# Layer 1 of a four-layer graph network: seven node tiles instead of six from neighbour lists for the last two batches, and their projections between quarters of the scored sums

## The chip, the cores and the metric

The kernel runs on one core of a Trainium2 chip. The core has five engines that work side by side, each with its own queue in which it goes in order: TensorE (PE, matrix products; its weight loads are shown apart as PEld), VectorE (DVE), ScalarE (ACT), GpSimd (POOL) and SyncE (SP, which here issues DMAs). They wait for each other by semaphores. The metric is the device time of one execution, in microseconds, as a median over several executions.

## What is computed

16 batches of N = 1024 nodes with D = 256 features pass four graph layers, all float32. The adjacency `adj` (1024 x 1024) is symmetric in its pattern and sparse: a node has a link to itself and to each other node with a chance of about 1.6%.

```python
# layer 0, per batch; U = h @ W1[:d], V = h @ W1[d:]
S = sigmoid(relu(U[u] + V[v] + b1) @ W2 + b2)            # one score per pair of nodes
a = (S * adj).T @ h ;  m = (adj.T @ h) * h
h = beta1*h + beta2*(a @ Wa + ba) + beta3*(m @ Wm + bm)
# layer 1
h = h + relu((adj @ h) @ W.T + b)
# layers 2 and 3, attention
feats = h @ W1.T ;  f = feats @ W2 + b2
h = softmax(leaky_relu(f[:, None] + f[None, :]) + adj) @ feats + bias2 + h
```

## The kernel before: how the work is tiled and ordered

**State and tiles.** The node state `z` of a batch lies feature-major in SBUF: 128 partitions x 2 feature halves x 1024 nodes. A node tile is P = 128 nodes, so there are NT = 8. Batches go in groups of GB = 4; there are NGR = 4 groups, `g` = 0 to 3. `product` (L131) is the one place that issues matrix products; one float32 product shows as two PE records, each with a weight load. A transpose by PE is one record.

**Layer 0** needs scores for linked pairs only. Neighbour lists name up to FIRST = 16 neighbours per node in a first table, and NG = 4 references to extra rows for nodes with more; the extra rows stand in XT = 6 tiles of 128 rows of QUAD = 4 neighbours each. Scores are worked out from gathered rows on POOL, DVE and ACT, in the background of PE's work on earlier groups (`side`), and put into a dense array in DRAM.

**The scored sums** of a group are in `with_edges` (L1118). They go over four quarters of the columns (QN = 256 nodes). A quarter takes eight PSUM banks `acc` (4 batches x 2 feature halves), loads a block `gd` of scores for each of eight node tiles, turns it into batch-major form `gc` (ACT L1133 for even tiles, DVE L1131 for odd), and issues eight products for each. At the quarter's end eight DVE additions (L1156) put the sums onto `z`. PSUM has eight banks in all, handed out in turn.

**Layer 1** for two batches at a time (`layer_one`, L1205): `projected` (L1161) makes `y` = `z` @ W.T node-major, in four steps of two node tiles (a step is two batches x two tiles x two feature halves = 8 products, 16 PE records), each bank copied out by ACT (L1174). `neighbours` (L1189) then sums `adj` @ `y` over a range of columns: for each of eight node tiles it loads a strip `adjT_in` by SP (L1195, three buffers) and issues four products. `onto` (L1181) applies relu on ACT (`r`, L1186) and adds to `z` on DVE (L1187).

**Layers 2 and 3** for two batches at a time (`pair_layers`): `front` makes `feats` and the two factors of the exponentials; `sums` builds for each node tile a weight matrix `m` by one DVE instruction (L1099), and issues four products with it; `second` and `third` scale by the row sums (reciprocal `share` on DVE, L1276 and L1330), turn back by transposes (L1289, L1316) and add.

**The last group's last two batches.** After `with_edges` of group 3, `far_ahead` (L1405) runs. It first projects batches 14 and 15 (`z[2:]`), and as each bank is copied out, SP stores it to `y_d` in DRAM (L1408; eight stores). From then on two things go side by side:
- the main line: `rest`, which is `neighbours` for batches 14 and 15 over the node columns from FAR x 128 on, then all layers of batches 12 and 13 (`pair_layers` with `layer_one`);
- `by_lists` (L1210), which makes the layer 1 sums of batches 14 and 15 for the first FAR node tiles from the neighbour lists: no PE, but for each list position a gather of 128 rows of 512 values from `y_d` by POOL (in `gather`, L708) and a DVE step that adds the scaled row to `msg` (L1246 for the first position, L1248 for the others). First come the 6 x 4 = 24 extra-row steps (`x_node`), whose sums `part` are stored by SP to `part_d` (L1252). Then come 16 steps for each of the FAR tiles, and last four steps for each tile that gather from `part_d` and add with an L1244 instruction.

Gathers run LEAD = 4 steps ahead of the DVE step that uses them, into slot buffers of which there are six. `slots` sets the pace: the generators of the main line yield their nominal PE time, and for each us of it 0.68 steps of `by_lists` are issued up to 82 us, and 0.61 after that. A DVE step made by `paced` also waits for the sixth-last PE product before it. Afterwards `from_lists` (L1255) turns `msg` back by transposes (L1265, four for each tile), `onto` adds it, and batches 14 and 15 go through layers 2 and 3, up to the kernel's end.

So the order on each engine is that of the program text after this interleaving; each engine goes through its own queue in order.

Of the kernel before, what the change touches and what calls it, by code (L numbers as in the profile page):

```python
# [29 lines left out]
NG = EXTRA // QUAD  # L30
XT = 6
HOLD = 40
FAR = 6
AHEAD = 3
LEAD = 4
TOP = 16.0
# [34 lines left out]
def gnn_stack_kernel(  # L71
# [616 lines left out]
    with tc.If(listed > 0) as arm:  # L688
        with ExitStack() as stack:
# [427 lines left out]
            def exponential(jt):  # L1117
                paced(nc.scalar.activation(ea[:, jt, :], ea[:, jt, :], AF.Exp), 16)  # L1118

            def with_edges(g, hw, z):  # L1120

                doing[0] = "edges"
                for v in range(N // QN):
                    cols = slice(v * QN, (v + 1) * QN)
                    acc = [[bank() for _ in range(DH)] for _ in range(GB)]
                    for ut in range(NT):
                        gd = first_gd.pop(0) if first_gd else load_gd(g, v, ut, back=BACK)
                        gc = gc_pool.tile([P, GB, QN], F32, tag="gc", name="gc")
                        by_batch = gd.rearrange("p n i -> p i n")
                        if ut % 2:  # L1130
                            paced(nc.vector.tensor_copy(gc, by_batch), 16)  # L1131
                        else:
                            paced(nc.scalar.activation(gc, by_batch, AF.Copy), 16)  # L1133
                        for i in range(GB):
                            for eh in range(DH):
                                product(
                                    acc[i][eh][:, :QN], hw[i][:, ut, eh * P : (eh + 1) * P], gc[:, i, :],
                                    start=ut == 0, stop=ut == NT - 1,
                                )
                        if z_loads and ut % 2 == 0:  # L1140
                            load, i = z_loads.pop(0)
                            paced(load(i), 12)
                        if (to_load or to_exp) and ut % 2 and v:
                            if v > 1 and to_exp:
                                exponential(to_exp.pop(0))
                            if to_load:
                                jt = to_load.pop(0)
                                paced(nc.sync.dma_start(ea[:, jt, :], adjT_d[jt]), 16)
                                to_exp.append(jt)
                        yield 3.4 if g or v else 1  # L1150
                    if v == N // QN - 1:
                        while to_exp:
# [8 lines left out]
            def projected(z, keep=None):  # L1161

                doing[0] = "one"
                y = [node_major("y") for _ in range(2)]
                for jt in range(0, NT, 2):
                    for i in range(2):
                        ps = bank()
                        for k in range(2):
                            for dh in range(DH):
                                product(  # L1170
                                    ps[:, k * D : (k + 1) * D], z[i][:, dh, (jt + k) * P : (jt + k + 1) * P],
                                    l1wT[:, dh, :], start=dh == 0, stop=dh == DH - 1,
                                )
                        nc.scalar.activation(  # L1174
                            y[i][:, jt : jt + 2, :], ps.rearrange("p (t d) -> p t d", t=2), AF.Copy
                        )
                        if keep:
                            keep(i, slice(jt, jt + 2), y[i][:, jt : jt + 2, :])
                        yield 1.7
                return y  # L1180

            def onto(z, cols, sums):
# [6 lines left out]
            def neighbours(y, z, cols):  # L1189
                doing[0] = "one"  # L1190
                n = cols.stop - cols.start
                acc = [[bank() for _ in range(DH)] for _ in range(2)]
                for jt in range(NT):
                    a = three.tile([P, HN], F32, tag="a", name="adjT_in")[:, :n]
                    nc.sync.dma_start(a, adjT_d[jt][:, cols])  # L1195
                    for i in range(2):
                        for eh in range(DH):
                            product(
                                acc[i][eh][:, :n], y[i][:, jt, eh * P : (eh + 1) * P], a,
                                start=jt == 0, stop=jt == NT - 1,  # L1200
                            )
# [9 lines left out]
            def by_lists(msg):  # L1211

                spares = [gd_pool.tile([P, QN, GB], F32, tag="gd", name="msg") for _ in range(4)]
                halves = [
                    t.rearrange("p n i -> p (n i)")[:, k * 2 * D : (k + 1) * 2 * D] for t in spares for k in range(2)
                ]
                msg.extend(halves[:FAR])
                part = halves[FAR:]
                nc.gpsimd.memset(part[0], 0.0)
                nc.sync.dma_start(part_d[XT * P :, :], part[0])  # L1220

                nc.vector.tensor_scalar(to_u, to_u, float(XT * P), None, ALU.min)
# [12 lines left out]

                for step in todo[:LEAD]:
                    fetch_row(*step)
                for n, (t, k) in enumerate(todo):
                    if n + LEAD < len(todo):
                        fetch_row(*todo[n + LEAD])  # L1240
                    z = got.pop((t, k))
                    to = msg[t] if t < NT else part[t % len(part)]
                    if t < NT and k >= FIRST:
                        paced(nc.vector.tensor_tensor(to, to, z, ALU.add))  # L1244
                    elif k == 0:
                        paced(nc.vector.tensor_scalar(to, z, lists(t)[3][:, k : k + 1], None, ALU.mult))  # L1246
                    else:
                        paced(nc.vector.scalar_tensor_tensor(  # L1248
                            to, z, lists(t)[3][:, k : k + 1], to, ALU.mult, ALU.add
                        ))  # L1250
# [173 lines left out]
            for g in range(NGR):  # L1424
                hw, z = loaded.pop(0)
                while g not in finished:
                    next(side.steps)
                side.along(with_edges(g, hw, z))
                if g < NGR - 1:
                    side.along(group_layers(g, z))  # L1430
                else:
                    for _ in far_ahead(z[2:], pair_layers(g * GB, z[:2], layer_one(z[:2]))):
# [134 lines left out]
```

## Time and profile before

| what | value |
|---|---|
| median of 6 executions | 3139.49 us (3132.43 to 3148.79) |
| the profiled execution: its time | 3140.89 us |
| the profiled execution: its span | 3139.1 us |
| mean granted TensorE clock in it | 0.996 |
| PE `gc,hw` products of group 3 end | 2724 us after the span's start |
| projections of batches 14 and 15 on PE | 2723.95 to 2737.8 us |
| `rest` (256 columns) on PE | 2737.8 to 2752.3 us |
| layer 1 of batches 12 and 13 on PE | 2752.3 to 2828.8 us |
| layers 2 and 3 of batches 12 and 13 on PE | 2828.8 to 2979.9 us |
| turning `msg` back on PE (24 transposes) | 2979.9 to 2982.5 us |
| first gather from `y_d`, last gather from `part_d` (POOL) | 2741.5 and 2970.6 us |

The profile is of one execution. Times are in microseconds from the start of its span; a line names engine, line of the kernel, operation, the buffers that it writes and reads, and how often. "Idle before" is the time in which the engine did nothing just ahead of the instruction, and the name behind the arrow is what released it ("issue" is no wait that the profile shows). In rows of groups the columns are: count, busy time, mean duration in ns, idle time before with its releasers.

### The profile page before, as it was taken

The numbers are of one execution on the slowest core, as the hardware profiler recorded it, in microseconds if no ns is written. First come the engines' busy times: TensorE is split into PE (matmuls) and PEld (weight loads), VectorE is DVE, ScalarE is ACT, GpSimd is POOL, SyncE is SP. The second block draws the span as 40 slices with busy tenths as digits, with TensorE's granted clock in tenths as the row PEclk, the third lists the DMA queues.
The fourth block names the chain that finished last, engine by engine and source line by source line (L and its number), as shares of the span: only waits on it lengthen the run. The fifth ranks groups of instructions, "written<-read, shape, count | busy, mean of one in ns | idle before, by whom it ended". The sixth has DMA issues, their size and how long they took to land. (4 is left out here: it accounts for less than half of the span.)

```text
span 3139.1 us, 39040 instructions
## 1 busy us (share of the span) xinstructions
PE 3080.7 (98%) x11954; PEld 2185.0 (70%) x11954; DVE 2423.3 (77%) x3247; ACT 1822.7 (58%) x6456; POOL 1886.3 (60%) x1483
## 2 busy tenths in 40 slices
PE   9999999999999999999999999999999999999999
PEld 5544544545547756888885688888568888858888
DVE  7887768678776779989887899988789982257844
ACT  3345555566665776767666677776667762214242
POOL 1156777676665677657667766667777651066600
PEclk9999999999999999999999999999999999999999
DMA  9998898888889777558877755797775564485500
GB/s 319 331 332 303 274 294 273 262 248 256 253 285 337 229 222 209 152 147 270 290 227 222 225 150 158 264 300 241 223 205 150 164 210 153 132 253 161 161 4 28
DMA packets 288420, 699.96 MB, mean 223 GB/s; under 512 B 46141, under 2 KB 141178, under 8 KB 281034
## 3 DMA queue, kind: packets, MB, share of 16 engines
q0 software_dynamic: 128224, 387.80, 42.3%
q1 hardware_dynamic: 132538, 258.46, 23.6%
q10 hardware_dynamic: 27440, 51.13, 4.3%
q8 instruction: 96, 1.57, 0.2%
q14 instruction: 122, 1.00, 0.1%
HBM read 565.83 MB, written 131.41 MB: 222 GB/s over the span
## 5 line engine op out<-in xcount | busy, mean ns | idle before, releaser
L831 ACT ACTIVATE z<-z 128x256 f32<-128x256 f32 x2432 | 979.3, 406 | 587.1 <-DVE z L827 507.8
L825 DVE TENSOR_TENSOR z<-z,u 128x1024 f32<-128x1024 f32 x608 | 737.5, 1219 | 301.4 <-PE bank L131 178.5
L131 PE MATMUL bank<-feats,m 128*128 128x257 f32 x4096 | 910.3, 380 | 5.5 <-ACT st L1329 4.6
L708 POOL DMA_INDIRECT z<-v_d,slot_v x512 | 662.5, 1294 | 385.0 <-ACT z L831 198.2
L131 PEld LDWEIGHTS bank<-feats,m 128*128 128x128 f32 x4096 | 770.6, 190 | 116.2 <-ACT st L1329 5.4
L713 POOL DMA_INDIRECT dense_d<-gt,slot_at x512 | 677.1, 1322 | 199.0 <-issue 140.9
L827 DVE SCALAR_TENSOR_TENSOR z<-z,w2r 128x1024 f32<-128x1024 f32 x608 | 737.1, 1219 | 9.3
L131 PE MATMUL bank<-gc,hw 128*128 128x256 f32 x2048 | 454.8, 383 | 19.4 <-ACT gc L1133 12.1
L831 ACT ACTIVATION_READ_ACCUMULATOR z<-z 128x1 f32 x2432 | 460.5, 189 | 0.6 <-issue 0.6
L131 PEld LDWEIGHTS bank<-gc,hw 128*128 128x128 f32 x2048 | 389.6, 192 | 84.1 <-ACT gc L1133 15.6
L131 PE MATMUL bank<-adj_sb,h 128*128 128x512 f32 x1024 | 442.4, 592 | 3.8 <-ACT st L333 1.9
L1099 DVE SCALAR_TENSOR_TENSOR m<-rho,tau,adj_sb 128x512 f32<-128x512 f32 x512 | 375.5, 742 | 69.7 <-PE bank L131 65.2
L131 PE MATMUL bank<-adjT_in,y 128*128 128x512 f32 (+1 forms) x960 | 401.4, 578 | 2.7 <-DMA adjT_in<-adjT_d 2.3
L131 PEld LDWEIGHTS bank<-adj_sb,h 128*128 128x128 f32 x1024 | 194.2, 190 | 243.5 <-issue 238.2
L131 PE MATMUL bank<-w,hT 128*128 128x512 f32 (+1 forms) x1024 | 335.0, 487 | 0.0
L131 PEld LDWEIGHTS bank<-adjT_in,y 128*128 128x128 f32 x960 | 181.6, 190 | 216.0 <-issue 204.0
L131 PEld LDWEIGHTS bank<-w,hT 128*128 128x128 f32 x1024 | 194.8, 191 | 141.5 <-issue 122.3
L1133 ACT ACTIVATE gc<-gd 128x1024 f32<-128x1024 f32 x64 | 132.9, 2077 | 178.9 <-PE bank L131 117.9
L131 PE MATMUL bank<-g_wT,z 128*128 128x257 f32 x1024 | 230.1, 380 | 0.0
L131 PEld LDWEIGHTS bank<-g_wT,z 128*128 128x128 f32 x1024 | 192.2, 190 | 30.0 <-issue 2.9
L708 POOL DMA_INDIRECT z<-v_d,x_node x96 | 126.3, 1316 | 121.6 <-ACT z L831 64.3
L1131 DVE COPY gc<-gd 128x1024 f32<-128x1024 f32 x64 | 71.4, 1116 | 109.4 <-PE bank L131 76.3
(169 smaller groups left out, 2442.9 us busy)
## 6 DMA issues: line engine op xcount, KB each, us to landing
gd<-dense_d SPq DMA_DIRECT2D x128, 512.0 KB
dense_d<-zero ACTq DMA_DIRECT2D x64, 512.0 KB
adjT_in<-adjT_d SPq DMA_DIRECT2D x112, 256.0 KB
h<-in_x_dram SPq DMA_DIRECT2D x19, 1024.0 KB
u_d<-st SPq DMA_DIRECT2D x64, 256.0 KB
v_d<-st SPq DMA_DIRECT2D x64, 256.0 KB
hw_d<-st SPq DMA_DIRECT2D x64, 256.0 KB
u<-u_d POOLq DMA_DIRECT2D x32, 512.0 KB
```

Source lines behind the costliest of these rows:

```text
L131: recent.append(nc.tensor.matmul(*args, **kw))
L708: return nc.gpsimd.indirect_dma_start(out=dst, out_offset=None, in_=src[:], in_offset=bass.IndirectOffsetOnAxis(ap=at, axis=0), **how,)
L713: return nc.gpsimd.indirect_dma_start(out=dst[:], out_offset=bass.IndirectOffsetOnAxis(ap=at, axis=0), in_=src, in_offset=None,)
L825: paced(nc.vector.tensor_tensor(z, z, u, ALU.add))
L827: nc.vector.scalar_tensor_tensor(zk, zk, 0.0, w2r[:, None, :].to_broadcast([P, GB, D]), ALU.max, ALU.mult)
L831: nc.scalar.activation(zk[:, c, :], zk[:, c, :], AF.Copy, accum_out=s[:, k, c : c + 1])
L1099: nc.vector.scalar_tensor_tensor(m, r[:, cols], ta[:, kt : kt + 1], ea[:, kt, cols], ALU.max, ALU.mult)
L1131: paced(nc.vector.tensor_copy(gc, by_batch), 16)
L1133: paced(nc.scalar.activation(gc, by_batch, AF.Copy), 16)
```

## The change

1. FAR goes from 6 to 7: seven node tiles of batches 14 and 15 come from lists, and `rest` has 128 columns instead of 256. That is 20 more gathers and DVE steps (16 from `y_d`, 4 from `part_d`), and 28 transposes in `from_lists`, whose second group has 384 columns instead of 256.
2. The two `part` tiles, which were spare halves of the four `msg` buffers, lie in a buffer of the `gc` pool.
3. The order of steps: for each tile its 16 rows from `y_d` and then its four from `part_d`, instead of all tiles' rows first and all parts last.
4. The stores of `part` to `part_d` are issued three steps later than the step that completes them.
5. The pace is 0.75 steps for each nominal us throughout.
6. The projection becomes a class whose `y` lies in two halves of node tiles (each for both batches) instead of one buffer for each batch. In group 3, `with_edges` gets it as `between`: projection step 0 runs after the second quarter, step 1 after the third, each with its two `y_d` stores. Steps 2 and 3 run at the start of `far_ahead`, after the fourth quarter.

```diff
-FAR = 6
+FAR = 7
...
-            def with_edges(g, hw, z):
+            def with_edges(g, hw, z, between=None):
...
+                    if between and 0 < v < N // QN - 1:
+                        yield from between(v - 1)
+
+            class Projection:
+                def __init__(self, z, keep=None):
+                    self.z, self.keep, self.halves = z, keep, []
+
+                def __call__(self, i, jt):
+                    return self.halves[jt // HT][:, i, jt % HT, :]
+
+                def pair(self, q):
+                    if q % 2 == 0:
+                        t = ttile("y")[:, : 2 * HT * D]
+                        self.halves.append(t.rearrange("p (i t d) -> p i t d", i=2, t=HT))
                     for i in range(2):
                         ps = bank()
                         for k in range(2):
+                            jt = 2 * q + k
                             for dh in range(DH):
                                 product(
...
+                        at = 2 * q % HT
+                        y = self.halves[-1][:, i, at : at + 2, :]
+                        nc.scalar.activation(y, ps.rearrange("p (t d) -> p t d", t=2), AF.Copy)
+                        if self.keep:
+                            self.keep(i, slice(2 * q, 2 * q + 2), y)
                         yield 1.7
...
-                part = halves[FAR:]
+                free = gc_pool.tile([P, GB, QN], F32, tag="gc", name="part").rearrange("p i n -> p (i n)")
+                part = [free[:, : 2 * D], free[:, 2 * D :]]
...
-                todo += [(t, k) for t in range(FAR) for k in range(FIRST)]
-                todo += [(t, FIRST + q) for t in range(FAR) for q in range(NG)]
-                got = {}
+                todo += [(t, k) for t in range(FAR) for k in range(FIRST + NG)]
+                got, done = {}, []
...
                     if t >= NT and k == QUAD - 1:
-                        nc.sync.dma_start(part_d[(t - NT) * P : (t - NT + 1) * P, :], to)
+                        done.append((n + 3, t - NT, to))
+                    if done and n == done[0][0]:
+                        _, at, of = done.pop(0)
+                        nc.sync.dma_start(part_d[at * P : (at + 1) * P, :], of)
...
-            def far_ahead(z, main):
-                both = y_d.rearrange("(t p) (i d) -> p t i d", p=P, i=2)
-                y = yield from projected(z, lambda i, ts, y: nc.sync.dma_start(both[:, ts, i, :], y))
+            def far_ahead(z, y, main):
+                doing[0] = "one"
+                for q in range(NT // 2 - 2, NT // 2):
+                    yield from y.pair(q)
                 gone, far = 0.0, Side(by_lists(msg))
                 rest = neighbours(y, z, slice(FAR * P, N))
...
-                        yield us * (0.68 if gone < 82 else 0.61)
+                        yield us * 0.75
...
-                side.along(with_edges(g, hw, z))
+                y = None
+                if g == NGR - 1:
+                    both = y_d.rearrange("(t p) (i d) -> p t i d", p=P, i=2)
+                    y = Projection(z[2:], lambda i, ts, y: nc.sync.dma_start(both[:, ts, i, :], y))
+                side.along(with_edges(g, hw, z, y and y.pair))
```

More of the change, by code (lines that the diff above doesn't have):

```diff
@@ L1159, in with_edges @@
                             )
[L1161 to L1165, printed above, removed]
+                    if between and 0 < v < N // QN - 1:
[9 more added lines that the diff above has]
+                        self.halves.append(t.rearrange("p (i t d) -> p i t d", i=2, t=HT))
                     for i in range(2):
@@ L1168, in projected @@
                         for k in range(2):
+                            jt = 2 * q + k
                             for dh in range(DH):
                                 product(
-                                    ps[:, k * D : (k + 1) * D], z[i][:, dh, (jt + k) * P : (jt + k + 1) * P],
+                                    ps[:, k * D : (k + 1) * D], self.z[i][:, dh, jt * P : (jt + 1) * P],
                                     l1wT[:, dh, :], start=dh == 0, stop=dh == DH - 1,
                                 )
[L1174 to L1178, printed above, removed]
-                        yield 1.7
+                        at = 2 * q % HT
[3 more added lines that the diff above has]
+                            self.keep(i, slice(2 * q, 2 * q + 2), y)
+                        yield 1.7
+            def projected(z):
+                doing[0] = "one"
+                y = Projection(z)
+                for q in range(NT // 2):
+                    yield from y.pair(q)
                 return y
@@ L1198, in neighbours @@
                             product(
-                                acc[i][eh][:, :n], y[i][:, jt, eh * P : (eh + 1) * P], a,
+                                acc[i][eh][:, :n], y(i, jt)[:, eh * P : (eh + 1) * P], a,
                                 start=jt == 0, stop=jt == NT - 1,
@@ L1403, in soon @@
                     first_gd.extend(load_gd(g, 0, ut) for ut in range(4))
-            def far_ahead(z, main):
-                both = y_d.rearrange("(t p) (i d) -> p t i d", p=P, i=2)
-                y = yield from projected(z, lambda i, ts, y: nc.sync.dma_start(both[:, ts, i, :], y))
+            def far_ahead(z, y, main):
+                doing[0] = "one"
+                for q in range(NT // 2 - 2, NT // 2):
+                    yield from y.pair(q)
                 gone, far = 0.0, Side(by_lists(msg))
@@ L1431, in gnn_stack_kernel @@
                 else:
-                    for _ in far_ahead(z[2:], pair_layers(g * GB, z[:2], layer_one(z[:2]))):
+                    for _ in far_ahead(z[2:], y, pair_layers(g * GB, z[:2], layer_one(z[:2]))):
                         pass
```

## The prediction, made before the result was known

> **What bounds the kernel now.** I began with the page's first part, busy time by engine, and with the line of granted clocks beside it.
>
> ```profile
> PE 3080.7 (98%) x11954; PEld 2185.0 (70%) x11954; DVE 2423.3 (77%) x3247; ACT 1822.7 (58%) x6456; POOL 1886.3 (60%) x1483
> ...
> PEclk9999999999999999999999999999999999999999
> ```
>
> TensorE (PE) is busy for 98% of the span at full clock, so only a removed PE instruction, or a removed PE gap, shortens the kernel; PEld (weight loads) runs beside it. The chain of waits holds only the last stores and says nothing here. The question is thus local: is PE still what ends last in the stretch that the change touches? The PE timeline of the last group gives that stretch.
>
> ```profile
> 2723.95 13.98 PE L131 MATMUL bank<-l1wT,z 128*128 128x256 f32 x64
> 2737.77 10.52 PE L131 MATMUL bank<-adjT_in,y 128*128 128x256 f32 x48
> ...
> 2760.38 0.38 PE L131 MATMUL bank<-l1wT,z 128*128 128x256 f32 x1 [0.83 <-issue]
> 2762.49 0.38 PE L131 MATMUL bank<-l1wT,z 128*128 128x256 f32 x1 [1.74 <-issue]
> 2763.90 9.55 PE L131 MATMUL bank<-l1wT,z 128*128 128x256 f32 x29 [1.03 <-issue]
> ...
> 2979.91 2.78 PE L1265 MATMUL bank<-ident,msg 128*128 128x128 f32 x24
> ```
>
> Columns are start, length, engine and line, operation, and in brackets the idle time before. The projections of the last two batches end at 2737.8, `rest` runs from there, and the turning back of `msg` (24 transposes) ends at 2982.5. There is one disturbance, around 2760. Beside this stretch POOL fetches neighbour rows; its groups for the whole stretch are these.
>
> ```profile
> L708 POOL DMA_INDIRECT z<-y_d,slot_v x96 | 107.4, 1118 | 45.8 <-DVE msg L1248 23.8 <-issue 18.3 <-DVE share L1276 1.2
> L708 POOL DMA_INDIRECT z<-part_d,to_u x24 | 30.4, 1268 | 11.6 <-DVE msg L1244 4.2 <-issue 3.4 <-DVE msg L1248 2.8
> L708 POOL DMA_INDIRECT z<-y_d,x_node x24 | 24.4, 1016 | 42.5 <-DMA y_d<-y 31.9 <-issue 5.0 <-DVE msg L1248 4.1
> ```
>
> The columns are busy us, mean ns of one, then idle time with its releasers. The 144 gathers are busy for 162 us, and every one is followed by at least 0.30 us:
>
> ```profile
> 2741.48 0.98 POOL L708 DMA_INDIRECT z<-y_d,x_node  x1 [31.91 <-DMA y_d<-y]
> ...
> 2744.49 0.95 POOL L708 DMA_INDIRECT z<-y_d,x_node  x1 [0.30 <-issue]
> ```
>
> So 144 gathers need 162 + 43 = 205 us of the 229 us between the first (2741.5) and the last (2970.6). POOL has some 24 us in hand: PE bounds the stretch, POOL is close behind. Last, the windows show how hard each engine is pressed in the neighbours (first row) and in the sums of layer 2 (second).
>
> ```profile
> core 0: us, PE busy (x) PEld busy (x) DVE busy (x) ACT busy (x) POOL busy (x), PEclk, DMA share, GB/s
> 2776.00:2829.00 53.00, 52.64 (x124) 23.14 (x123) 29.76 (x42) 4.81 (x7) 37.65 (x36) 1.00 0.80 252
> 2845.00:2889.00 44.00, 43.32 (x213) 37.88 (x212) 39.09 (x72) 10.83 (x27) 30.66 (x27) 1.00 0.57 158
> ```
>
> In the sums VectorE (DVE) is already busy for 39.09 of 44 us, 0.89.
>
> **The change, part by part.**
>
> *Rest, 256 to 128 columns.* It keeps 64 PE records. At 256 columns one costs (2752.26 − 2737.77 − 0.45 idle) / 64 = 0.219 us. No f32 product of 128 columns of this kind is in the trace: at best 0.109 (the 24 transposes of 128 columns, 2.62 us), at worst the old 0.219. I take 0.11, near the transposes, which have the same width: 64 × 0.109 = **7.0 us less**. Four more transposes cost 0.4. PE saves 6.6 us (0 to 6.6).
>
> *Seventh tile by lists.* 16 + 4 more gathers on POOL and as many DVE steps: 164 instead of 144. Where do they fit? The first gather waits for the last `y_d` store, which follows projections 2 and 3. In the changed order of PE these still end the projections, after the same number of products, so at the same 2737.8: the first gather stays at 2741.5. From there I add up POOL, each gather with its 0.30 behind it:
> - 24 extra rows at 1.016 + 0.30: 31.6 us.
> - In the program order of DVE 65 steps stand ahead of the first `m` of the first sums. The other 41 are 33 `y_d` rows beside the neighbours, where the trace has 1.062 (pitch 1.365, 45.0 us), and 8 part rows, which before come only later: between 1.06 and 1.27, taken 1.12 (pitch 1.42, 11.4 us).
> - The remaining 99 go beside fronts and sums: 79 at 1.161 (second window: 27 took 31.3 us), pitch 1.464, 115.7 us; 20 part rows at 1.27, pitch 1.57, 31.5 us.
>
> Together 235 us, so the last gather starts at about 2975. From a gather's start to its DVE step the trace has 3.7 us, the step takes 0.75, the last transposes 0.4 to 3: the turning back ends at 2980 to 2982.5, against 2982.5 before. PE alone would be there at 2982.5 − 6.6 = 2976, or at 2969 if the disturbance goes too. So **POOL ends last, and the 6.6 us are mostly eaten**. An `m` (L1099) stands in DVE's queue behind gather steps, and PE's sums wait for `m`; that is how POOL's lateness reaches PE.
>
> *Bubbles.* When POOL and PE wait for each other through DVE, each DVE operation that waits for PE delays a gather. Before, the reciprocals `share` (L1276) cost POOL 0.9 us over three sums; 8 sums give 2.4 us. I take that, 0 to 5.
>
> *Pace 0.68/0.61 to 0.75.* It costs nothing itself, but asks one step per 1.33 us of nominal PE time, less than any pitch above: 11 steps in one sums of 14.8 us instead of 9. Gathers cannot follow at 1.46. At the first sums (PE would be there by 2830) the 65th step is not before 2832 to 2834, so PE waits some 2 to 4 us; this is in POOL's sum already.
>
> *Projections 0 and 1 between quarters.* A permutation of PE's work: 16 records each, 3.5 us, earlier by 30 to 60 us. Before, no PE gap is at these boundaries, so none is filled. Their banks come free while the quarter's other products still run, since the 8 banks end one after another over 3.4 us. Their evacuation on ACT may stand behind one copy of `gc` (2.08 us) and is wanted 2.6 us later: 0 to +1 us for both, taken 0. The four early stores on SP pass behind `gd` loads that are wanted 5 us later or more: 0. The stores of part sums go three steps later, and a DVE step that writes that tile again follows two steps (2.7 us) on: 0 to +3 us, taken 0, as six slot buffers stand between DVE and POOL. On SP three of them come one after another ahead of an `adjT_in` load that PE wants at about the same time (bound: +2 us, taken 0). `part` in a `gc` buffer, free once the edges end: 0.
>
> *Sum.* End of the turning back −2.1 (middle of −2.5 and 0, nearer the first, since most transposes need only early tiles), bubbles +2.4: **+0.3 us**. Against the profiled execution (span 3139.1, time 3140.9; the median of six is 3139.5, 1.4 lower) that gives 3141.2, and by the median 3139.8. I say **3140**.
>
> *A rule against the trace.* In the trace a gather takes 0.95 us while DVE is idle, 1.16 in the sums and 1.27 beside the two-input additions of L1244. The Trainium skill, page "SBUF — State Buffer", section "Who interferes with whom", holds that a DVE addition whose two inputs lie in SBUF takes only the shared pair's read interface, while descriptor generation needs the write interface (called inferred there), so that a GpSimd DMA should not suffer from it. By that rule all 164 gathers would keep a pitch of 1.25 us, 205 us in all, POOL would be done by 2947, and PE would keep the end. The rows disagree with it (1.27 against 0.95), and I go by the rows.
>
> **Rivals.**
>
> *PE stays the bound.* For it: POOL's idle time before is mostly waiting for DVE steps that are held back to PE's pace, and at a pitch of 1.40 or less throughout, the 164 are done by 2971. PE then saves 6.6, and if the disturbance around 2760 (3.6 us of gaps, then 6.8 us at half clock, 3.4 lost) does not return, 13.6. Time 3127 to 3133. Against: that pitch was seen only beside the neighbours. Whether the disturbance comes back I can't tell; its releaser is "issue".
>
> *The gathers slow down further (the slower side).* The mechanism is DVE density in layer 2's sums: 6 more steps in 44 us at 0.67 make DVE 39.1 + 4.0 = 43.1 of 44 us busy. The rows give 0.95 at no DVE work, 1.06 at 0.56 busy, 1.16 at 0.89; going on to 1.0 gives about 1.20 to 1.29. At 1.29 the 79 gathers cost 10 us more, the part rows 1.5 more, and PE gaps of 3 us and over halve the clock as at 2612, where the window after a 3.7 us gap has PEclk 0.60, 1.6 us lost. Then +0.3 + 10 + 1.5 + 1.6 = +13: 3153. It decides from a mean pitch of 1.56 in the sums (9 us / 99 = 0.09 over the row). Against: as POOL becomes the bound the sums stretch, and DVE's density falls back to about 0.92.
>
> *The move does nothing.* If the projections between quarters bring nothing, as I reckon, the seventh tile is the whole effect; the forecast has this in it. Were the gathers to begin some 7 us earlier through it, the forecast becomes 3133.
>
> **How the numbers follow.** Forecast 0.47, all within 0.3% (9.4 us, about what a measurement of this kernel can tell from no change). PE stays the bound 0.25: 0.20 faster, 0.05 within. Gathers slow down 0.28: 0.25 slower, 0.03 within. Faster 0.20, same 0.55, slower 0.25. The range takes in both rivals' main prices, 3128 to 3152.
>
> **What would show it.** Right: the first gather near 2741.5 after the same projections, POOL pitch about 1.46 in the sums with nearly no idle time beyond 0.30, PE gaps released by DVE `m` L1099 (2 to 4 us at the first sums, then small ones), `rest` about 7 us shorter, and the turning back ending within 5 us of 2982.5. Wrong: PE without gaps in the sums (PE bound), a pitch of 1.56 or more (the slower rival), gathers starting well before 2741, or a new gap at a quarter's boundary.

## The result and the profile after

The changed kernel takes 3150.57 us (median of 20, 3141.74 to 3159.04), the kernel before 3137.7 (median of 46). The ratio is 1.0042 with a 95% interval of 1.0031 to 1.0053: slower by some 13 us. The profiled execution after has a span of 3144.0 us and a time of 3145.68.

The loss stands in the stretch that the change touches. Counted from the first list gather (2741.5 before, 2731.3 after) to the end of the turning back of `msg` (2982.5 and 2987.1), the stretch takes 241.0 us before and 255.8 after. That is 14.7 us more, where the forecast had 238.5 to 241 and bubbles of 2.4. The second pair of layers behind it takes PE 150.5 us before and 150.8 after. The spans of the two profiled executions differ by 4.9 us only, because the one after reached its first list gather 10.2 us earlier. That is no gain of the change: the same program text ahead of the stretch reaches it at 2731.3 in one execution and at 2741.2 in another (after and run 4), at 2741.5 and 2746.3 (before and run 2). So single executions are compared by the stretch alone.

First the busy times of the page after.

```profile
PE 3081.2 (98%) x11958; PEld 2180.9 (69%) x11958; DVE 2435.0 (77%) x3267; ACT 1821.3 (58%) x6456; POOL 1915.1 (61%) x1503
```

PE's busy time is as before although 7 us of work went, so PE must be running slower, or longer, somewhere. The windows of the stretch show where: `rest` with the projections of batches 12 and 13, the 512-column neighbours, the fronts (the matrix products that make `feats`), the sums; first the four of before, then the four of after.

```profile
core 0: us, PE busy (x) PEld busy (x) DVE busy (x) ACT busy (x) POOL busy (x), PEclk, DMA share, GB/s
2737.80:2773.20 35.40, 31.24 (x129) 25.91 (x128) 13.57 (x22) 6.33 (x12) 21.73 (x22) 0.90 0.74 232
2773.20:2828.80 55.60, 55.24 (x130) 24.30 (x129) 31.07 (x44) 5.37 (x8) 39.81 (x38) 1.00 0.79 249
2828.80:2844.10 15.30, 15.09 (x75) 12.93 (x73) 8.13 (x17) 9.36 (x24) 10.26 (x11) 1.00 0.63 180
2844.10:2979.90 135.80, 135.12 (x667) 118.53 (x668) 112.62 (x204) 43.06 (x100) 90.39 (x76) 1.00 0.56 159
```

```profile
2727.60:2748.50 20.90, 20.90 (x129) 19.20 (x128) 6.02 (x12) 4.34 (x9) 13.04 (x13) 1.00 0.73 228
2748.50:2815.50 67.00, 58.94 (x129) 25.28 (x129) 35.29 (x52) 4.92 (x8) 49.10 (x47) 0.95 0.81 251
2815.50:2835.30 19.80, 17.13 (x75) 14.10 (x74) 12.88 (x24) 10.29 (x25) 13.19 (x12) 0.91 0.54 154
2835.30:2983.80 148.50, 142.35 (x668) 119.39 (x667) 120.94 (x218) 42.36 (x100) 102.65 (x95) 0.98 0.64 180
```

The first window has no gap: 20.9 us, against 35.4 before (14.5 for `rest` and 20.9 for the projections with their disturbance). Then the stretch pays it back twice: the neighbours take 67.0 instead of 55.6 us, the fronts 19.8 instead of 15.3, the sums 148.5 instead of 135.8. Each of these three windows has a granted clock below 1. The PE timeline of the second window shows what happens.

```profile
2744.64 4.05 PE L131 MATMUL bank<-l1wT,z 128*128 128x256 f32 x18
2748.53 2.74 PE L131 MATMUL bank<-adjT_in,y 128*128 128x512 f32 x6
2751.84 0.59 PE L131 MATMUL bank<-adjT_in,y 128*128 128x512 f32 x1 [0.57 <-issue]
2753.97 0.59 PE L131 MATMUL bank<-adjT_in,y 128*128 128x512 f32 x1 [1.54 <-issue]
2755.39 8.61 PE L131 MATMUL bank<-adjT_in,y 128*128 128x512 f32 x16 [0.84 <-issue]
2765.95 3.70 PE L131 MATMUL bank<-adjT_in,y 128*128 128x512 f32 x8 [1.95 <-DMA adjT_in<-adjT_d]
2772.81 2.90 PE L131 MATMUL bank<-adjT_in,y 128*128 128x512 f32 x3 [3.16 <-issue]
```

Two kinds of gaps stand here. The disturbance that had been around 2760 before came again, around 2752. It is followed by two gaps in which PE waits for `adjT_in` (the second shows as "issue"; its products stand behind the load that SP issues at 2766.77). The two kinds have different causes, and the experiments ask what each is worth.

**The first kind: signals of PE that arrive late.** PE ended its last projection product at 2748.7. ACT copies each bank out as soon as PE signals it:

```profile
2741.10 0.60 ACT L1188 ACTIVATE y<-bank 128x512 f32<-128x512 f32 x1 [1.60 <-PE bank L131]
2745.43 0.60 ACT L1188 ACTIVATE y<-bank 128x512 f32<-128x512 f32 x1 [3.74 <-PE bank L131]
2752.58 0.60 ACT L1188 ACTIVATE y<-bank 128x512 f32<-128x512 f32 x1 [6.55 <-PE bank L131]
2757.59 1.57 ACT L1188 ACTIVATE y<-bank 128x512 f32<-128x512 f32 x3 [4.41 <-PE bank L131]
```

A bank takes PE 1.73 us, so the last four banks were done at about 2743.5, 2745.2, 2747.0 and 2748.7. ACT, which had nothing else to do, began to copy them at 2752.58 and from 2757.59 on: 9 and 12 us late. DVE steps that wait for the same signals stand still, gathers stop behind them, and PE comes to products that need the copies. The same holds at 2818.9 (the `r` of the last neighbours, 6 us late), at 2888 to 2896 (copies of `feats`, up to 8.5 us late) and at 2930. In the trace of before this is the disturbance around 2760; in its sums there is none. The bank that ACT copies at 2764.66 had been done 10.5 us earlier:

```profile
2764.66 2.65 ACT L1174 ACTIVATE y<-bank 128x512 f32<-128x512 f32 x5 [7.40 <-PE bank L131]
```

The ends of products in a profile are modelled, so the products themselves might have been late. The traces also hold the time at which each recorded semaphore update (the signal by which one engine tells the others that it has finished) took place, and that decides it. In the profile after, PE ends nine signalling products between 2745.41 and 2752.56, and no update of its semaphore is recorded in between; from 2757.53 to 2758.07 thirteen stand 0.04 to 0.07 us apart, although one such product takes PE 0.43 us or more. So the signals were held up, not the products. ACT starts within 0.03 us of the updates at 2752.56 and 2757.57.

I call an update of PE late when it stands over 0.1 us behind the end of PE's latest signalling product. From 2700 us to the end of the stretch there are 31 of them in the trace of before and 136 after. Further ahead, in the earlier groups, there are 111 and 81, so the fault was in the kernel before as well, in places that the change doesn't touch. The recorded updates of ACT and DVE in the stretch are at most 0.02 us late.

**The second kind: loads behind stores.** SP's queue in the same time:

```profile
2742.08 0.37 SPq L1213 DMA_DIRECT2D adjT_in<-adjT_d  x1
2748.78 12.08 SPq L1273 DMA_DIRECT2D part_d<-part  x3
2760.96 0.37 SPq L1213 DMA_DIRECT2D adjT_in<-adjT_d  x1
2766.35 0.32 SPq L1273 DMA_DIRECT2D part_d<-part  x1
2766.77 0.90 SPq L1213 DMA_DIRECT2D adjT_in<-adjT_d  x2
```

Three stores of part sums stand one after another and wait for DVE, and DVE for gathers and late signals. The next `adjT_in` load goes out only at 2760.96, and PE wants it at 2764.0. The fifth store holds up the next one until 2766.77.

### The profile page after: what moved, and what is told of

It is laid out like the page before. It is cut to its first block, busy times and chain, and to the rows that moved or that the text cites. A ratio compares the mean times of both kernels' runs of the same rounds, so it can differ in the third digit from the quotient of the medians.

```text
span 3144.0 us, 39121 instructions
## 1 busy us (share of the span) xinstructions
PE 3081.2 (98%) x11958; PEld 2180.9 (69%) x11958; DVE 2435.0 (77%) x3267; ACT 1821.3 (58%) x6456; POOL 1915.1 (61%) x1503
## 5 line engine op out<-in xcount | busy, mean ns | idle before, releaser
L1099 DVE SCALAR_TENSOR_TENSOR m<-rho,tau,adj_sb 128x512 f32<-128x512 f32 x512 | 375.7, 742 | 71.0 <-PE bank L131 65.0
```

What stands on the lines that cost most here:

```text
L1099: nc.vector.scalar_tensor_tensor(m, r[:, cols], ta[:, kt : kt + 1], ea[:, kt, cols], ALU.max, ALU.mult)
```

## The experiments

Four theories, by the letters that the expectations use. **A**: PE's signals come late where gathers follow each other densely. **B**: POOL's sum of gather times sets the end (the forecast). **C**: the density of DVE's steps or of any transfers does it. **D**: the part stores on SP hold up `adjT_in`. Runs 1 to 4 were made on one chip, 5 to 8 and 12 on a second, 9 to 11 on a third, each beside runs of the kernel before on the same chip; ratios are to those. The kernel before took 3141.44 us beside runs 1 to 4, 3125.47 beside 5 to 8, 3125.70 beside 9 to 11 and 3124.09 beside 12. On which chip the profiles before and after were taken is not on record. The difference between chips turned out to matter.

**1. The move alone** (six tiles, old pace, old order of steps, part tiles and stores).

```diff
-FAR = 7
+FAR = 6
...
-                        yield us * 0.75
+                        yield us * (0.68 if gone < 82 else 0.61)
```

> Theory A (signals of PE reach DVE and ACT late once POOL issues gathers back to back, and PE then stands still and loses its clock): six tiles, old pace, so the gathers are as dense as before; the same as before, 3138 within 4 us. Theory B (POOL has simply too many gathers, its sum of durations sets the end): the same as before too, 3138 within 4. If the projections between the quarters are themselves the cost: 3145 or more. If they bring a gain that the seventh tile then eats: 3131 or less.

Ratio 1.0003 (0.9987 to 1.0018). The projections between the quarters are worth nothing, as costed, and PE has no gap at the quarters' boundaries. The stretch is 242.3 us.

**2. The pace alone.**

```diff
-                        yield us * (0.68 if gone < 82 else 0.61)
+                        yield us * 0.75
```

> Six tiles in the old order, only the pace is 0.75. Theory A: the 144 gathers stand closer together, so PE's signals are late in the sums too and the kernel is slower than before by 5 to 12 us (3143 to 3150), with new PE gaps released by ACT or DVE after late signals. Theory B: the same number of gathers, POOL has 24 us in hand; no slower than before, 3134 to 3139.

Ratio 1.0062 (1.0040 to 1.0083): 19 us slower, with the same gathers as before and no seventh tile. Theory B said no slower; it falls as the only cause. The trace shows late signals in the projections and, unlike before, in the sums. This is ACT where the `feats` of a batch for layer 3 are copied (2.42 us of waiting ahead of one copy; the product that it copies had ended some 7 us before), and PE right behind it:

```profile
2914.33 0.39 ACT L1016 ACTIVATE feats<-bank 128x257 f32<-128x257 f32 x1 [2.42 <-remote]
```

```profile
2914.77 0.70 PE L131 MATMUL bank<-feats,m 128*128 128x257 f32 x2 [2.10 <-ACT feats L1016]
2916.22 0.91 PE L131 MATMUL bank<-feats,m 128*128 128x257 f32 x2 [0.74 <-ACT feats L1016]
```

PE's product waits for a copy, the copy for a signal of PE: short gaps in a row, then a half-clock window. The stretch is 260.6 us, 19.6 more than before, as much as the ratio says. From 2700 us on it has 100 late updates of PE, where before has 31.

**3. The seventh tile without the move.**

```diff
-                side.along(with_edges(g, hw, z, y and y.pair))
+                side.along(with_edges(g, hw, z))
...
-                for q in range(NT // 2 - 2, NT // 2):
+                for q in range(NT // 2):
```

> The changed kernel with all four projection steps after the fourth quarter. Theories A and B: as the changed kernel, 3150 within 4 us. If the move were the cost: 3140 or less.

Ratio 1.0050 (1.0034 to 1.0066), as the changed kernel (1.0042). If the parts simply add, the move is worth 0, the pace about +19 us, and the seventh tile with its new order of steps about −4 to −6, since everything but the move comes to +13 to 16. That would be nearly what PE's sum says (6.6 us), but it isn't shown: the interval of run 2 alone reaches from 13 to 26 us, and no run has the seventh tile at the old pace. The trace has 121 late updates from 2700 us on.

**4. Spacers on POOL.**

```diff
                         gather(z, y_d, lists(t)[1][:, k : k + 1])
+                        nc.gpsimd.memset(spacer, 0.0)
```

(the same behind the gathers from `part_d`)

> The changed kernel with a 128x128 memset on POOL after each gather of the lists, which sets the smallest pitch at about 1.4 us instead of 1.25. Theory A: the late signals go or shrink, and the kernel is faster than the changed one by 4 to 10 us (3140 to 3146), although POOL has more to do. Theory B: POOL has 15 to 25 us more to do and is the bound; slower than the changed kernel by 10 us or more (3160 or more).

Ratio 1.0125 (1.0105 to 1.0146), which is what B expected, but the kernel didn't do what it was made for. Nothing ties a spacer to its gather, and the program order has them in bunches of up to 12. So gathers still follow each other at 1.25 us, with pauses between, and POOL spends 34 us on the spacers (10 of them ahead of the first gather). The stretch takes 281.8 us, and PE pays most of that in one place:

```profile
2850.39 7.67 PE L131 MATMUL bank<-g_wT,z 128*128 128x257 f32 x24 [24.73 <-DVE z L1205]
```

The addition of layer 1's sums (L1205) stands in DVE's queue behind list steps whose gathers are late. That is a path from POOL over DVE to PE, as in the forecast, but by this addition and not by `m`. It tells nothing about A: the gathers weren't spaced, and 83 late updates stand from 2700 us on.

**5. Plain loads instead of gathers.** On the second chip.

```diff
-                        gather(z, part_d, to_u[:, at : at + 1])
+                        nc.gpsimd.dma_start(z, part_d[t % XT * P : (t % XT + 1) * P, :])
...
-                        gather(z, y_d, lists(t)[1][:, k : k + 1])
+                        nc.gpsimd.dma_start(z, y_d[k % NT * P : (k % NT + 1) * P, :])
```

> The changed kernel whose list gathers are plain loads of 128 consecutive rows from POOL's queue: the same bytes into the same buffers, the same DVE steps, pace and PE work, but not the listed rows (so the lists' sums are of other rows). Theory A (dense indirect gathers make PE's signals late): no late signals, PE bounds the stretch and has 6.6 us less and no disturbance around 2760: 3125 to 3132. Theory C (it is the density of DVE's steps or of the transfers, with any kind of DMA): 3145 or more, with late signals as before. Theory B (POOL's gather time alone) would also give 3125 to 3132, but says nothing of late signals.

Ratio 0.9960 (0.9945 to 0.9974), 12.5 us faster than before. POOL's share of a row falls to 0.54 us:

```profile
L1252 POOL DMA_DIRECT2D z<-y_d x130 | 69.8, 538 | 119.9 <-DVE msg L1266 60.3 <-DVE msg L1262 18.4 <-DVE part L1266 14.3
```

POOL now waits for DVE, and PE runs through: 221.58 us busy of 221.90 between 2720.7 and 2942.6, at clock 1.00. On this chip the same DVE steps and the same bytes cost nothing. That does not refute theory C, because the unaltered kernel has no late signals on this chip either (run 12). The gain is in the range of the PE-bound rival (6.6 to 13.6 us), with rows that hold POOL for half as long as a gather.

**6. Spacing that holds.** A small memset into the slot itself, which the gather has to follow.

```diff
+                        nc.gpsimd.memset(z[:, :32], 0.0)
                         gather(z, y_d, lists(t)[1][:, k : k + 1])
```

(the same ahead of the gathers from `part_d`)

> The changed kernel with a small memset (128x32) on POOL into the slot ahead of each list gather, which the gather has to follow, so no two gathers follow each other at 1.25 us (pitch 1.40 to 1.55). Theory A: hardly any late signals from PE; what POOL loses against the pace of 0.75 is paid instead, so 3145 to 3160. Theory B: POOL has 0.15 to 0.3 us more for each of 164 gathers, 25 to 50 us: 3170 or more.

Ratio 1.0033 (1.0020 to 1.0046). No update of PE is late, but neither is one in run 12, which has no memset on the same chip; so this is no gain of the spacing. The trace has gaps ahead of `adjT_in` (4.09, 1.02 and 1.78 us) and waits for DVE operations behind list steps (2.89 and 2.95 us ahead of PE's L1067). The memset is 0.14 us for each of 164 gathers, 23 us of POOL, of which 12 arrive in the time (1.0033 against 0.9995 of run 12).

**7. The same spacing in the kernel before.** Edit as in 6.

> The kernel before (six tiles, pace 0.68 and 0.61) with the same memset ahead of each list gather. Theory A: the disturbance around 2760 (7 us of gaps and half clock) goes or shrinks: 3131 to 3137. Theory B: as before or slower, 3138 to 3150.

Ratio 1.0008 (0.9997 to 1.0019). No late signals and no disturbance, but not faster, so theory A's number missed. Run 12 has no late signals on this chip without any memset, so this run can't tell what the disturbance costs where it occurs. Theory D's gap stands there:

```profile
2764.39 6.14 PE L131 MATMUL bank<-adjT_in,y 128*128 128x512 f32 x8 [5.79 <-DMA adjT_in<-adjT_d]
```

On SP three stores of part sums stand from 2746.39 to 2758.84 ahead of the load, issued at 2758.95, that PE wants at 2758.6. In the trace of before, without the memset, the largest gap ahead of `adjT_in` is 0.36 us.

**8. Five tiles.**

```diff
-FAR = 7
+FAR = 5
...
-                        yield us * 0.75
+                        yield us * 0.57
```

> The changed kernel with five tiles by lists and a pace of 0.57: 124 gathers, 384 columns in rest. PE has 7 us more than before and 14 more than the changed kernel. Theory A: few late signals, so about the PE sum: 3138 to 3146, faster than the changed kernel. If the number of tiles alone counted (PE's work): 3157 to 3165, slower than the changed kernel.

Ratio 1.0009 (0.9999 to 1.0019): about 3 us slower than before. One gap of 3.44 us ahead of `adjT_in`, with a half-clock window; otherwise PE is the bound, with 54.9, 14.9 and 135.4 us for neighbours, fronts and sums.

**9. Part stores on POOL's queue.** On the third chip.

```diff
-                        nc.sync.dma_start(part_d[at * P : (at + 1) * P, :], of)
+                        nc.gpsimd.dma_start(part_d[at * P : (at + 1) * P, :], of)
```

> The changed kernel with the stores of part sums issued from POOL's queue instead of SP's. Theory D (the stores wait on SP for DVE's part sums, and adjT_in loads stand behind them): the two gaps of 1.95 and 3.16 us ahead of adjT_in products around 2765 and 2770 go, and one half-clock window with them; 5 to 8 us faster than the changed kernel, so 5 to 9 us slower than before (ratio 1.0015 to 1.003). Theory A alone (late signals of PE behind dense gathers carry all of the loss): within 3 us of the changed kernel, ratio 1.0035 to 1.005.

Ratio 0.9999 (0.9990 to 1.0008). The gaps ahead of `adjT_in` are gone, the neighbours take 54.9 us. But PE, early now, stops at the next place, behind the 56th list step:

```profile
2810.07 7.10 PE L131 MATMUL bank<-g_wT,z 128*128 128x257 f32 x24 [7.18 <-DVE z L1205]
```

DVE's timeline ahead of that addition shows why: every list step waits for its gather.

```profile
2805.47 0.75 DVE L1266 SCALAR_TENSOR_TENSOR msg<-z,slot_a,msg 128x512 f32<-128x512 f32 x1 [0.26 <-DMA z<-y_d,slot_v]
2807.14 0.75 DVE L1266 SCALAR_TENSOR_TENSOR msg<-z,slot_a,msg 128x512 f32<-128x512 f32 x1 [0.92 <-DMA z<-y_d,slot_v]
2808.66 0.75 DVE L1266 SCALAR_TENSOR_TENSOR msg<-z,slot_a,msg 128x512 f32<-128x512 f32 x1 [0.77 <-DMA z<-y_d,slot_v]
2809.33 1.29 DVE L1205 TENSOR_TENSOR z<-z,r 128x512 f32<-128x512 f32 x2
```

Taken alone, this would look as if the stores carried all of the loss. Run 12 shows that they don't: on such a chip there is no loss to remove.

**10. Both mends in the kernel before** (the memset of 6 and the stores of 9).

> The kernel before with the 128x32 memset ahead of each list gather, and with the stores of part sums on POOL's queue. Theories A and D together: neither the disturbance around 2760 nor the gap ahead of adjT_in that took its place when the gathers were spaced alone; 5 to 9 us faster than before (ratio 0.997 to 0.9985). If the spaced gathers lose their gain to DVE's queue: as before, 0.999 to 1.001.

Ratio 1.0004 (0.9995 to 1.0014). Neither disturbance nor `adjT_in` gap, and in their place one gap of 7.30 us ahead of the fronts, released by DVE's `z` L1187. The hoped-for version that beats both is not this one.

**11. Five tiles with the stores on POOL** (edits of 8 and 9).

> Five tiles by lists, pace 0.57, stores of part sums on POOL's queue. With the stores on SP this had one gap of 3.4 us ahead of an adjT_in product and a half-clock window (1.7 us) and was 2.9 us slower than before. Theory D: both go, 1 to 3 us faster than before (ratio 0.999 to 0.9997). Otherwise as with the stores on SP: 1.0009.

Ratio 0.9998 (0.9987 to 1.0010): the gap and its half-clock window are gone, and it is even with before. Between this and run 8 lie 3.4 us by the medians over those of before, where the trace of 8 showed 3.44 + 1.7; but the intervals overlap, and the chips differ.

**12. The changed kernel again, unaltered.** On the second chip, that of runs 5 to 8.

> The changed kernel once more, unaltered, on the chip that comes: the kernel before took 3141 us on the chip of the first four runs and 3125 on those of the later ones, and the late signals of PE (ACT and DVE waiting up to 12 us for a product that had ended) were seen only in the former. Theory D (stores of part sums on SP hold up the adjT_in loads): the ratio to before is 1.003 to 1.005 on any chip, with the gaps ahead of adjT_in products, and the run with the stores on POOL (0.9999) shows what they cost. Theory A (late signals carry the loss): on a chip where before takes about 3125, no late signals and a ratio of 0.999 to 1.0015; on one where it takes about 3140, 1.004.

Ratio 0.9995 (0.9982 to 1.0008). **On this chip the change makes no difference.** The two traces of one program can be laid side by side. ACT's copies of the last four projection banks:

```profile
2740.98 0.60 ACT L1188 ACTIVATE y<-bank 128x512 f32<-128x512 f32 x1 [1.13 <-PE bank L131]
2742.71 0.60 ACT L1188 ACTIVATE y<-bank 128x512 f32<-128x512 f32 x1 [1.13 <-PE bank L131]
2744.44 0.60 ACT L1188 ACTIVATE y<-bank 128x512 f32<-128x512 f32 x1 [1.13 <-PE bank L131]
2746.16 0.60 ACT L1188 ACTIVATE y<-bank 128x512 f32<-128x512 f32 x1 [1.13 <-PE bank L131]
```

One copy every 1.73 us, the last of them 0.04 us after PE's last projection product (2746.12). And PE:

```profile
2741.64 4.48 PE L131 MATMUL bank<-l1wT,z 128*128 128x256 f32 x20
2745.96 10.46 PE L131 MATMUL bank<-adjT_in,y 128*128 128x512 f32 x24
2760.46 5.32 PE L131 MATMUL bank<-adjT_in,y 128*128 128x512 f32 x8 [4.03 <-DMA adjT_in<-adjT_d]
2766.64 7.10 PE L131 MATMUL bank<-adjT_in,y 128*128 128x512 f32 x16 [0.87 <-DMA adjT_in<-adjT_d]
...
2919.29 0.32 PE L1067 MATMUL bank<-ident,top 128*128 128x128 f32 x1 [2.93 <-DVE top L1023]
```

The disturbance is gone, the gap behind the stores on SP is there on this chip too. The windows:

```profile
2746.00:2808.40 62.40, 57.21 (x129) 24.75 (x128) 36.03 (x53) 5.33 (x8) 47.20 (x47) 0.97 0.85 270
2808.40:2823.30 14.90, 14.90 (x74) 13.09 (x73) 10.94 (x21) 9.02 (x23) 11.55 (x12) 1.00 0.72 197
2823.30:2962.00 138.70, 135.68 (x669) 118.68 (x669) 122.34 (x221) 43.26 (x101) 104.02 (x95) 1.00 0.69 193
```

Against the profile of the result: 4.6 us less in the neighbours, 4.9 in the fronts, 9.8 in the sums; the stretch is 236.3 instead of 255.8 us. The gathers are just as dense in both (95 in the last window, busy 102.65 and 104.02 us). So it is not the work that differs but the late signals (136 against none), and with them the gaps and the half clock.

## Why the prediction was right, and where it was not

The measured time lies in the range (3128 to 3152), near its upper end, and that is in part luck: the upper end was the price of the slower rival, whose mechanism did not come, and the late signals that took the time are in no term of the sum. The likeliest case, no difference, did not come true in the result (+0.42%), and did on the chip of run 12 (−0.05%). One sign came by luck too: the turning back ends within 5 us of 2982.5 only because this execution was 10.2 us ahead when the stretch began.

- *Move: 0.* Right (run 1 at 1.0003, run 3 as the changed kernel). The first gather starts 3.8 us after the projections end (2727.6, 2731.3), before 3.7.
- *Rest: −7.0 us, at 0.11 for a record of 128 columns.* Right: 24 records in 2.84 us, the last one overlapping, are 0.112 each.
- *POOL's sum: 235 us.* Too high by 8. The groups of the stretch after are these:

```profile
L708 POOL DMA_INDIRECT z<-y_d,slot_v x112 | 121.9, 1089 | 47.6 <-issue 25.7 <-DVE msg L1266 12.4 <-DVE msg L1264 3.2
L708 POOL DMA_INDIRECT z<-part_d,to_u x28 | 31.2, 1114 | 12.2 <-issue 6.5 <-DVE msg L1266 4.8 <-DVE share L1297 0.3
L708 POOL DMA_INDIRECT z<-y_d,x_node x24 | 24.9, 1036 | 23.5 <-DMA y_d<-y 13.3 <-issue 6.3 <-DVE part L1264 3.0
```

  178 us busy and 164 times 0.30 are 227. Gathers in the sums took 1.08 us instead of the 1.16 that I carried over, and it wasn't that DVE had less to do: between 2828 and 2872 us of run 12, in the same sums, DVE is busy for 41.49 of 44 us (0.94, where the row of 1.16 had 0.89), and a gather takes 1.12. The gathers of part rows took 1.11, not 1.27, and 1.11 as well in run 2, which keeps the order of before with the additions of L1244 in a row. So my reading that these additions make a gather slow was not confirmed. The rule of the Trainium skill that I set aside there (page "SBUF — State Buffer", section "Who interferes with whom": such an addition should not slow a GpSimd DMA) stands better than I held. But gathers beside busy DVE still took more than the 0.95 of an idle one.
- *POOL takes up PE's gain.* Right in kind on the later chips: taking POOL's gather time away (run 5) frees 12.5 us, and taking away one wait (run 9) only moves it, from the gap behind SP's stores to the addition L1205 behind list steps. The path was another than forecast. PE does not wait at the first sums for `m` behind the 65th step, but some steps earlier for L1205 (7 us in run 9); the gaps that `m` L1099 releases in the profile after are 0.41 and 0.59 us, not 2 to 4.
- *POOL ends last.* Not confirmed. In run 12, without late signals, the last gather starts 226.2 us after the first (forecast 233.5), and PE runs without a gap from 2919.45 to the end of the turning back, so PE ends last there. What takes PE's gain is waits on the way: 4.9 us behind SP's stores and 2.9 behind DVE's `top`, with 1.7 lost at half clock. In the profile after, the last gather starts 246.9 us after the first, behind late signals.
- *The slower rival* (gathers slow down with DVE's density, 3153). Its time nearly came, its mechanism did not: with its 0.30 us a gather in the sums takes 1.38 us, not 1.56. From start to start the gathers stand 1.53 us apart there, but the rest is waiting for DVE behind late signals; in run 12 it is 1.41 us with DVE busier.
- *The step that failed* is the pace: "It costs nothing itself". Alone it costs 19 us on the chip of the first runs (run 2), and it raises the late updates of PE from 31 to 100. The other is "Whether the disturbance comes back I can't tell; its releaser is 'issue'": I had the disturbance in hand as 7 us of the trace of before, and priced only that it might go, not that it might come more often. It ends with ACT waiting 7.4 us for a product that had ended 10.5 us ago, which the ACT timeline of before shows; I read only PE's.
- *SP: three stores ahead of an `adjT_in` load, bound +2, taken 0.* The place was right, the size was not: 4.9 us of gaps and a half-clock window (1.7) on the chip of run 12, 5.1 and 1.7 in the profile after. On the later chips it costs nothing in sum, because POOL would make PE wait a little later anyway (run 9).

**What stays open.** That the late signals carry the loss is shown by two comparisons: run 2 has more of them than before and takes 19 us more, and run 12 has the changed kernel without them and without the loss. Where they come from is not. Late updates of PE are in the traces of before, of after and of runs 1 to 4, and in none of the eight traces of runs 5 to 12, on two other chips; the unaltered kernel of run 12 has none. That they depend on the chip is the plainest reading, but runs 1 to 4 were also the first in time, and the first chip was not used again.

Two facts of the traces bear on it. Dense gathers go with the late signals: from 200 us on, each of the 1009 late updates in the six traces has at least four indirect DMAs of POOL in the 8 us before it, while 28% of the time has fewer than four. This fits theory A as a condition, but not as the whole cause, since run 12 issues its gathers at least as densely; and what else is dense in the same places (DVE's steps, the transfers) is not told apart, because the kernel without gathers ran only where there was nothing to see. Second, the six traces are incomplete: 12 to 14% of the updates of PE are not in them (3702 of 4298 in the profile after) and 13 to 17% of those of DVE and ACT, where the eight others have them all. So a further rival is that the recording of events itself holds up the signals there. Every execution here has a span and a clock on record, so none is known to have run without it. Nor was the pace alone tried on the later chips.

## What to carry to other kernels

Look at the engines that wait for a bound engine, not only at the bound engine's own gaps: a wait that goes on after the awaited product has ended is a fault that can grow, as it did here with a faster side stream (31 late signals, then 100). Before a side stream is made faster, ask which of its waits stand in a queue that the main line needs: here a store on SP ahead of a load, and a step on DVE ahead of an addition; when the first was taken away (run 9), the second took over. And compare only with runs on the same chip: the same kernel differed by 16 us between chips, more than the change did, and the change itself went from +0.42% to nothing.

## What the runs showed of the hardware

- PE's signals reached ACT up to 12.4 us after the product's end in the profile after, and up to 13.5 us in run 3; in run 12, for the same program as after, each recorded update of PE from 200 us on stands within 0.02 us of a product's end.
- The kernel before took 3141 us on one chip and 3124 to 3126 on two others. Its mean granted clock was 0.9955 there and 0.9971 to 0.9972 on the others. Some 13 us of that lie ahead of the stretch: the first list gather starts at 2731.3 to 2746.3 us (mean 2739.7) in the six traces with late signals, and at 2721.1 to 2731.5 (mean 2727.0) in those of runs 6 to 12.
- Three short gaps within 4.1 us (0.57, 1.54 and 0.84, in the second window after) were followed by 3.4 us at half clock, as was a single gap of 4.03 us in run 12. So the gap need not be in one piece. Single gaps of 2.95 us (run 6) and 2.93 us (run 12) were followed by a half-clock window and by none.
- A plain load of 128 rows of 2 KB takes POOL 0.54 us, a gather of as many listed rows 0.95 to 1.8 us, mostly 0.95 to 1.4, with 0.30 behind it.
